# Keys and queries of the first image copied from SBUF, and the residuals of the second layer loaded inside the block and summed in place

## The chip, the core and the metric

The kernel runs on one core of a Trainium2 chip. The metric is the device time of one execution in microseconds (us); less is better. The core has TensorE (PE, matrix products, with its weight loads shown apart as PEld), VectorE (DVE), ScalarE (ACT), GpSimd (POOL) and SyncE (SP). They run side by side, each through its own list of instructions in order, and wait for one another through semaphores. Transfers are issued from SP's and POOL's lists here, and a few from ACT's at the very start.

## What is computed

Two attention layers, one after the other, over 4 images of 64 x 64 positions (4096 tokens) with 256 channels, in float32. Cut to what matters:

```python
def layer0(x):                       # x: (4, 4096, 256)
    q, k, v = x @ Wq + bq, x @ Wk + bk, x @ Wv + bv      # widths 32, 32, 256
    attn = softmax(einsum('bnd,bmd->bnm', q, k), axis=-1)
    return gamma * einsum('bnm,bmc->bnc', attn, v) + x

def layer1(x):
    f, g, v = x @ Wf + bf, x @ Wg + bg, x @ Wh + bh      # widths 32, 32, 128
    beta = softmax(einsum('bqd,bkd->bqk', g, f), axis=-1)
    return x + (einsum('bqk,bkd->bqd', beta, v) @ Wo + bo)
```

## The kernel before

`fast_path` does the work; `general_path` is a fallback behind a flag and does not run here.

**Projections.** A block is 512 tokens, 8 per image. `project_units(b, l, j)` gives a list of small functions for block j of image b in layer l: transpose the tokens, project q and k (`qk_unit`, tile psqk), project v (`v_unit`, tile psv). To keep precision with the faster number type, a value is split into a high and a low part. `qk_unit` leaves q and k of a block in one SBUF tile, `qk_parts`, of 128 rows: high q, high k, low q, low k, 32 rows each. The pool holds one such tile. Line 428 writes it to DRAM (`qk_dram`), from SP.

**Repeating rows.** The score matmul contracts over 128 rows, which are q and k repeated: q as high, high, low, low and k as high, low, high, low, so that one matmul sums all four products. `load_q` (lines 465 to 470) and `load_k` (lines 472 to 477) read these 32-row pieces from `qk_dram` with four transfers of 64 KB each, issued from POOL. A k tile is kept for each of the 8 blocks; there are two q tiles.

**Steps.** The main loop runs over `Step`s. In the first layer 256 queries stand against 512 keys in a step: 16 blocks of queries with 8 steps each. In the second layer 512 queries stand against 256 keys: 8 blocks with 16 steps. `scores()` computes the score tile st, of which there is one, on PE (line 502), and its exponentials on ACT: p (line 514), and in split steps also high (line 512) with a small factor. `cut_low` and `cut_both` compute low (line 519) and d (line 524) on DVE. In the first layer every step is split, in the second layer steps 2, 7 and 12. `products_first` and `products_second` multiply by v into the acc tiles (lines 533 and 554). In the second layer DVE also sums p (p_sum, line 700). In the program, step n does the scores of step n+2 ahead of its own products.

**The end of a block.** `end_first` gives the residual functions of the first layer: they write the new x to DRAM twice, as x1_dram for the next transposes and as x1_res with the output bias added. `end_second` (line 597) gives the output functions of the second layer for a block of 512 queries. Before: `begin` loads two pieces of the residual x1_res (128 tokens each, tile x_old, line 612) from SP, an empty function follows, and then four times `output(t)`: a matmul with Wo and one with ones (tile pso, lines 623 and 624), a reciprocal (line 626), y from pso and x_old (line 628), a transfer to the output (line 630), and the load of residual t+2. All of these tiles come from `small`, a ring of four buffers which x_res and x_new of the first layer share. The side tiles in PSUM (psqk, psv, pso) share two buffers.

**Pacing.** These functions form the list `units` and are spread over the steps of the next block: by step i of a second-layer block, ceil(len(units) * (i + 1) / 11) of them are done (line 704), in the first layer over 7 steps. In image b's second layer the projections of image b+1 are appended to the same list.

**The start.** The first `AHEAD` = 3 blocks of image 0 are projected ahead of the loop, with `load_k` after each and `load_q` after the first. The other five are projected within the first five steps (lines 689 to 720), `load_k` coming after the projection.

**The order of instructions.** The tile framework reorders what the program says: for each engine it makes a list of its own, from its picture of when tiles are ready. So an edit that makes a tile ready earlier, or shortens `units`, moves instructions of other engines too.

Of the kernel before, what the change touches and what calls it, by code (L numbers as in the profile page):

```python
# [50 lines left out]
F32R = mybir.dt.float32r  # L51
I32 = mybir.dt.int32
AF = mybir.ActivationFunctionType
ALU = mybir.AluOpType
AX = mybir.AxisListType

P = 128
QB = 512
QB0 = 256
NT = QB // P  # L60
# [3 lines left out]
AHEAD = 3  # L64
# [169 lines left out]
def fast_path(ctx: ExitStack, tc: tile.TileContext, x, w0, w1, wo, bo, gamma, out, off):  # L234

    nc = tc.nc
    B, N, C = x.shape
    NCC = C // P
    NB = N // QB
    D = w0[0].shape[1]  # L240
# [5 lines left out]
    NI = (N // (G[0] * P), N // (G[1] * P))  # L246
# [56 lines left out]
    inverse = const.tile([P, 2, B * N // P], F32, name="inverse")  # L303
# [39 lines left out]
    for j in range(NB):  # L343
        forms = {}
        for what, col in (("h", 1.0), ("l", 0.0), ("d", -EPS)):
            t = const.tile([P, NT, W], F32R, name=f"v0{what}_{j}")
# [19 lines left out]
    xT, x_parts, k_t, v_t = {}, {}, {}, {}  # L366
    qk_dram, x1_dram, x1_res = {}, {}, {}
    q_t = {}
# [36 lines left out]
    def project_units(b, l, j):  # L405
        key = (b, l, j)

        def qk_unit():
            ps = side_psum(f"psqk_{b}_{l}_{j}")
            for c in range(NCC):  # L410
                for n in range(2):
                    nc.tensor.matmul(  # L412
                        ps,
                        wqk[l][:, c, :],
                        x_parts[key][c][n],
                        start=(c == n == 0),
                        stop=(c == NCC - 1 and n == 1),
                    )
            whole = data.tile([2 * D, QB], F32, tag="qk", name=f"qk_{b}_{l}_{j}")
            parts = data.tile([P, QB], F32R, tag="qk_parts", name=f"qk_parts_{b}_{l}_{j}")  # L420
            top, bottom = slice(0, 2 * D), slice(2 * D, P)
            nc.scalar.copy(whole, ps[bottom, :])  # L422
            nc.vector.scalar_tensor_tensor(whole, ps[top, :], bqk[l], whole, ALU.add, ALU.add)  # L423
            nc.scalar.copy(parts[top, :], whole)
            nc.vector.tensor_sub(parts[bottom, :], whole, parts[top, :].bitcast(F32))

            qk_dram[key] = dram.tile([2, 2, D, QB], F32, name=f"qk_dram_{b}_{l}_{j}")
            nc.sync.dma_start(qk_dram[key].rearrange("h w d n -> (h w d) n"), parts.bitcast(F32))

        per = QB // CV[l]  # L430

        def v_unit(t0):
            def issue():
                ps = side_psum(f"psv_{b}_{l}_{j}_{t0}").rearrange("p (t c) -> p t c", c=CV[l])
                for t in range(per):
                    for c in range(NCC):
                        nc.tensor.matmul(  # L437
                            ps[:, t, :],
                            xT[key][:, c, (t0 + t) * P : (t0 + t + 1) * P],
                            wv[l][:, c, :],  # L440
                            start=(c == 0),
                            stop=(c == NCC - 1),
                        )
                tiles = slice(t0, t0 + per)
                seen = [seen_v[:, l, b * NB + j, n : n + 1] for n in range(2)]
                if l == 0:
                    split_values(ps, *(v0[j][what][:, tiles, :C] for what in ("h", "l", "d")), seen[t0 // per])
                    return
                for n in range(NT // G[1]):
                    i = j * NT // G[1] + n  # L450
                    v = ps[:, n * G[1] : (n + 1) * G[1], :]
                    if split[1][i]:
                        t = data.tile([P, 3, G[1], P], F32R, tag="v1_parts", bufs=sum(split[1]), name=f"v_{b}_{i}")
                        v_t[b, i] = {what: t[:, m] for m, what in enumerate(("h", "l", "d"))}
                        split_values(v, *v_t[b, i].values(), seen[n])
                    else:
                        v_t[b, i] = data.tile([P, G[1], P], F32, tag="v1", bufs=V1, name=f"v_{b}_{i}")
                        nc.scalar.copy(v_t[b, i], v)
                        nc.scalar.activation(v, v, AF.Abs, accum_out=seen[n])

            return issue

        return [transpose_unit(b, l, j), qk_unit] + [v_unit(t0) for t0 in range(0, NT, per)]

    def load_q(b, l, j):

        q_t[b, l, j] = data.tile([P, QB], F32R, tag="q", bufs=2, name=f"q_{b}_{l}_{j}")
        for n in range(4):
            src = qk_dram[b, l, j][n // 2, 0].bitcast(F32R)
            nc.gpsimd.dma_start(q_t[b, l, j][n * D : (n + 1) * D, :], src)  # L470

    def load_k(b, l, j):

        k_t[b, l, j] = data.tile([P, QB], F32R, tag="k", bufs=NB, name=f"k_{b}_{l}_{j}")
        for n in range(4):
            src = qk_dram[b, l, j][n % 2, 1].bitcast(F32R)
            nc.gpsimd.dma_start(k_t[b, l, j][n * D : (n + 1) * D, :], src)  # L477

    def nothing():
        pass  # L480
# [1 line left out]
    def small(name):  # L482
        return work.tile([P, C], F32, tag="small", bufs=4, name=name)
# [79 lines left out]
    def end_first(b, j, acc):  # L563
# [30 lines left out]

        return [residual(0), residual(1)]

    def end_second(b, j, acc, p_sum):
        key = f"{b}_{j}"
        o = []
        for h in range(QB // QB0):  # L600
            part = slice(h * QB0, (h + 1) * QB0)
            o.append(work.tile([P, W], F32, tag="o", name=f"o_{key}_{h}"))
            nc.scalar.activation(o[h][:, :QB0], acc[0][:, part], AF.Copy, scale=1.0 + EPS)
            nc.vector.tensor_add(o[h][:, :QB0], o[h][:, :QB0], acc[1][:, part])
        sums = work.tile([P, QB], F32, tag="sums", bufs=1, name=f"sums_{key}")
        nc.vector.tensor_add(sums, p_sum[:, :QB], p_sum[:, QB:])
        x_old = {}

        def load(t):
            if t < NT:  # L610
                x_old[t] = small(f"x1_old_{key}_{t}")
                nc.sync.dma_start(x_old[t], x1_res[b, j][t * P : (t + 1) * P, :])

        def begin():
            load(0)
            load(1)

        def output(t):
            def issue():
                tok = slice(t * P, (t + 1) * P)  # L620
                ps = side_psum(f"pso_{key}_{t}")
                part = o[t // NS][:, t % NS * P : (t % NS + 1) * P]
                nc.tensor.matmul(ps[:, :C], part, wo_sb, start=True, stop=True)  # L623
                nc.tensor.matmul(ps[:, C : C + 1], sums[:, tok], ones[:, :1], start=True, stop=True)  # L624
                n = (b * N + j * QB) // P + t
                nc.vector.reciprocal(inverse[:, 1, n : n + 1], ps[:, C : C + 1])
                y = small(f"y_{key}_{t}")
                nc.vector.scalar_tensor_tensor(y, ps[:, :C], inverse[:, 1, n : n + 1], x_old[t], ALU.mult, ALU.add)  # L628
                row = j * QB + t * P
                nc.sync.dma_start(out[b, row : row + P, :], y)  # L630
                load(t + 2)

            return issue

        return [begin, nothing] + [output(t) for t in range(NT)]

    def run(units):
        for u in units:
            u()


    x_res = {}
    for j in range(AHEAD):
        run(project_units(0, 0, j))
        load_k(0, 0, j)
        if j == 0:
            load_q(0, 0, 0)

    steps = [Step(b, l, j, i) for b in range(B) for l in range(2) for j in range(NQ[l]) for i in range(NI[l])]
    steps[0].scores()  # L650
# [7 lines left out]
    for n, s in enumerate(steps):  # L658
        b, l, j = s.b, s.l, s.j
# [14 lines left out]
        if l == 0 and s.last:  # L674
            x_res[b, j] = []
            for t in range(NS):
                x_res[b, j].append(small(f"x_res_{b}_{j}_{t}"))
                row = (j * NS + t) * P
                nc.sync.dma_start(x_res[b, j][t], x[b, row : row + P, :])
                nc.gpsimd.tensor_add(x_res[b, j][t], x_res[b, j][t], bv)  # L680

        ahead = steps[n + 3] if n + 3 < len(steps) else None
        if ahead is not None and ahead.first:
# [5 lines left out]
        early = []  # L689
        if b == l == j == 0 and s.i + AHEAD < NB:  # L690
            early = project_units(0, 0, s.i + AHEAD)
# [17 lines left out]
        if l == 1:  # L709
            later.scores()  # L710
            run(todo)
            s.products_second(acc)
        else:
            for half, what in ((0, "h"), (0, "l"), (1, "h")) if s.last else ((0, "h"), (1, "h")):
                s.products_first(acc, half, what)
            for half in () if s.last else (0, 1):
                s.products_first(acc, half, "l")
            run(early[1:])
            if early:
                load_k(0, 0, s.i + AHEAD)  # L720
            later.scores()
            run(todo)
            for half, what in ((0, "d"), (1, "l"), (1, "d")) if s.last else ((0, "d"), (1, "d")):
                s.products_first(acc, half, what)
# [76 lines left out]
```

## Time and profile before

| | us |
|---|---|
| median of 3 runs | 3236.67 (3235.38 to 3236.88) |
| the profiled execution | 3232.45 |
| its span, from first to last instruction | 3230.6 |
| mean granted clock of PE | 0.997 of full |

Busy time of PE in the span is 3166.9 us. The costliest groups and some that matter here, one row each from the groups by line:

| line, engine, tile | number | mean ns |
|---|---|---|
| 514 ACT p | 1024 | 1020 |
| 512 ACT high | 608 | 1116 |
| 519 DVE low | 608 | 1329 |
| 524 DVE d | 608 | 1255 |
| 700 DVE p_sum | 480 | 1223 |
| 623 PE pso with Wo | 256 | 380 |
| 470 POOL issue of q | 256 | 503 |
| 477 POOL issue of k | 256 | 499 |

Transfers from issue to landing, median: x_old from x1_res 2.1 us (128 times, 128 KB), qk_dram from qk_parts 2.1 (64 times, 256 KB), k and q from qk_dram 2.1 each (256 times, 64 KB).

How to read it: a matmul's end is modelled and matmuls are pipelined, so a busy PE can hold short waits; the distance between starts in the timeline tells more. "Idle before" names the engine whose work ended a wait last. Starts are in us from the beginning of the span.

### The profile page before, as it was taken

The page shows a single profiled execution, that of the slowest core. Times are in us where ns is not written, and L with a number is a line of the kernel's source. Part 1 is how long each engine was busy: PE and PEld are TensorE (multiplying, and loading weights), DVE is VectorE, ACT ScalarE, POOL GpSimd, SP SyncE. Part 2 cuts the span into 40 slices and gives each one's busy share as a digit, 9 for nine tenths or more (in the row PEclk, how much of TensorE's full clock was granted, in tenths as well). Part 3 has the DMA queues.
Part 4 walks back from the last instruction along what each step waited for, and adds up shares of the span by engine and source line. Part 5 has one row for each costly group of instructions (what it writes and reads, how often), then busy time and mean ns, then how long its engine had stood idle before and what let it go on. Part 6 is the DMA issues. An engine that isn't in the chain of part 4 may idle for free. (4 is left out here: it accounts for less than half of the span.)

```text
span 3230.6 us, 51123 instructions
## 1 busy us (share of the span) xinstructions
PE 3166.9 (98%) x19460; PEld 2616.2 (81%) x19460; DVE 2686.0 (83%) x3181; ACT 1989.2 (62%) x2483; POOL 660.7 (20%) x784
## 2 busy tenths in 40 slices
PE   8999999999999999999999999999999999999998
PEld 6999997565699999656679999966668999995554
DVE  6788888888888888888888888878888888887776
ACT  6666666555566666565556666655555666665554
POOL 2222223000222222300022222310002222241000
PEclk9999999999999999999999999999999999999999
DMA  4112123222212112322121212222222211121111
GB/s 116 41 50 50 43 57 74 58 53 49 63 44 56 42 47 51 77 56 51 48 64 44 50 46 54 60 66 53 49 54 61 53 44 47 43 71 47 33 33 36
DMA packets 368652, 172.15 MB, mean 53 GB/s; under 512 B 257392, under 2 KB 343664, under 8 KB 368400
## 3 DMA queue, kind: packets, MB, share of 16 engines
q1 hardware_dynamic: 342528, 134.29, 16.0%
q0 software_dynamic: 24960, 34.18, 4.4%
q8 instruction: 157, 2.57, 0.3%
q14 instruction: 95, 0.78, 0.1%
q10 hardware_dynamic: 912, 0.33, 0.0%
HBM read 101.58 MB, written 67.11 MB: 52 GB/s over the span
## 5 line engine op out<-in xcount | busy, mean ns | idle before, releaser
L514 ACT ACTIVATE p<-st 128x1024 f32<-128x1024 f32 x1024 | 1044.5, 1020 | 386.3 <-PE st L502 380.1
L512 ACT ACTIVATE high<-st,down 128x1024 fp32r<-128x1024 f32 x608 | 678.7, 1116 | 691.4 <-PE st L502 571.0
L524 DVE SCALAR_TENSOR_TENSOR d<-low,high 128x1024 fp32r<-128x1024 f32 x608 | 762.9, 1255 | 208.7 <-PE acc L533 203.3
L519 DVE TENSOR_TENSOR low<-p,high 128x1024 fp32r<-128x1024 f32 x608 | 807.8, 1329 | 140.9 <-ACT p L514 140.9
L554 PE MATMUL acc<-p,v 128*128 128x512 f32 x1664 | 789.3, 597 | 0.0
L502 PE MATMUL st<-q,k 128*128 128x256 f32 (+1 forms) x3072 | 775.8, 361 | 11.7 <-ACT p L514 11.5
L700 DVE TENSOR_TENSOR p_sum<-p_sum,p 128x1024 f32<-128x1024 f32 x480 | 586.8, 1223 | 58.8 <-ACT p L514 50.8
L502 PEld LDWEIGHTS st<-q,k 128*128 128x128 f32 x3072 | 463.3, 189 | 208.4 <-ACT p L514 115.1
L533 PE MATMUL acc<-v0d,d 128*128 128x258 f32 x4096 | 592.3, 284 | 0.1
L533 PE MATMUL acc<-v0h,high 128*128 128x258 f32 x4096 | 588.6, 284 | 3.1 <-ACT high L512 3.0
L533 PE MATMUL acc<-v0l,low 128*128 128x258 f32 x4096 | 588.3, 283 | 2.3 <-DVE low L519 2.3
L533 PEld LDWEIGHTS acc<-v0h,high 128*128 128x128 f32 x4096 | 533.8, 190 | 5.3 <-ACT high L512 3.8
L533 PEld LDWEIGHTS acc<-v0d,d 128*128 128x128 f32 x4096 | 533.9, 190 | 4.8 <-DVE d L524 1.6
L533 PEld LDWEIGHTS acc<-v0l,low 128*128 128x128 f32 x4096 | 533.0, 190 | 3.9 <-DVE low L519 3.7
L554 PEld LDWEIGHTS acc<-p,v 128*128 128x128 f32 x1664 | 308.7, 190 | 226.0 <-issue 198.9
L590 POOL TENSOR_TENSOR x_res<-x,bo 128x256 f32<-128x256 f32 x128 | 215.2, 1681 | 858.6 <-DVE g L580 480.1
L470 POOL DMA_DIRECT2D q<-qk_dram x256 | 125.9, 503 | 1165.5 <-PE st L502 1145.1
L680 POOL TENSOR_TENSOR x_res<-x_res,bv 128x256 f32<-128x256 f32 x128 | 190.1, 1486 | 149.9 <-DMA x_res<-in_x 102.8
L437 PE MATMUL psv<-wv,xT 128*128 128x128 f32 (+1 forms) x1024 | 191.1, 330 | 7.5 <-DVE qk L423 6.7
L477 POOL DMA_DIRECT2D k<-qk_dram x256 | 125.1, 499 | 300.6 <-DMA qk_dram<-qk_parts 158.4
L437 PEld LDWEIGHTS psv<-wv,xT 128*128 128x128 f32 x1024 | 159.0, 192 | 29.6 <-DVE qk L423 9.3
L388 DVE TENSOR_TENSOR xl<-xT,xh 128x512 fp32r<-128x512 f32 x128 | 87.0, 683 | 4.0 <-ACT xh L387 3.7
(94 smaller groups left out, 1676.7 us busy)
## 6 DMA issues: line engine op xcount, KB each, us to landing
x_res<-in_x SPq DMA_DIRECT2D x128, 128.0 KB, 2.2
qk_dram<-qk_parts SPq DMA_DIRECT2D x64, 256.0 KB, 2.1
k<-qk_dram POOLq DMA_DIRECT2D x256, 64.0 KB, 2.1
q<-qk_dram POOLq DMA_DIRECT2D x256, 64.0 KB, 2.1
x_dram<-x SPq DMA_DIRECT2D x128, 128.0 KB, 1.7
x_res<-x_res SPq DMA_DIRECT2D x128, 128.0 KB, 1.7
squares<-x_dram SPq DMA_DIRECT2D x256, 64.0 KB, 2.3
x_old<-x_res SPq DMA_DIRECT2D x128, 128.0 KB, 2.1
```

Source lines behind the costliest of these rows:

```text
L437: nc.tensor.matmul(ps[:, t, :], xT[key][:, c, (t0 + t) * P : (t0 + t + 1) * P], wv[l][:, c, :], start=(c == 0), stop=(c == NCC - 1),)
L470: nc.gpsimd.dma_start(q_t[b, l, j][n * D : (n + 1) * D, :], src)
L502: nc.tensor.matmul(st[:, g, :], k_t[b, l, kt // NT][:, kt % NT * P : (kt % NT + 1) * P], q_t[b, l, j * n // QB][:, q0 : q0 + n], start=Tru ...
L512: nc.scalar.activation(self.high, s_flat, AF.Exp, bias=down)
L514: nc.scalar.activation(self.p, s_flat, AF.Exp)
L519: nc.vector.tensor_sub(self.low, self.p, self.high.bitcast(F32))
L524: nc.vector.scalar_tensor_tensor(self.d, self.low.bitcast(F32), -1.0 / EPS, self.high.bitcast(F32), ALU.mult, ALU.add)
L533: nc.tensor.matmul(acc[2 * s + which][:, :W], p[:, g * QB0 + s * P : g * QB0 + (s + 1) * P], v0[self.i][v][:, g, :], start=self.first and ...
L554: nc.tensor.matmul(acc[which], v[:, g, :], p[:, g * QB : (g + 1) * QB], start=first and g == 0, stop=last and g == G[1] - 1,)
L590: nc.gpsimd.tensor_add(x_old[s], x_new[s], bo_sb)
L680: nc.gpsimd.tensor_add(x_res[b, j][t], x_res[b, j][t], bv)
L700: nc.vector.tensor_add(p_sum, p_sum, s.p)
```

## The change

It has three parts.

1. For image 0 in the first layer, `qk_unit` itself calls `load_k` (and for block 0 `load_q`) right after the write to DRAM, with the tile `qk_parts` as the source in place of `qk_dram`. The write to DRAM stays; q tiles of later blocks are still read from it. The calls of `load_k` and `load_q` ahead of the loop and in it go. The two functions share a helper, `load_rows`.
2. In the second layer the four pieces of the residual are loaded by `load_old`, called at step 12 of 16 of the block that they belong to, in place of the loads at the end. `begin`, the empty function and the loads in `output` go, so that `end_second` gives four functions and not six.
3. y has no tile of its own: it is written over the residual, and goes out from there.

```diff
+            if b == l == 0:
+                near = parts.rearrange("(h w d) n -> h w d n", h=2, w=2)
+                load_k(b, l, j, near)
+                if j == 0:
+                    load_q(b, l, j, near)
...
-    def load_q(b, l, j):
-
+    def load_rows(dst, parts, which, halves):
+        for n, h in enumerate(halves):
+            nc.gpsimd.dma_start(dst[n * D : (n + 1) * D, :], parts[h, which])
+
+    def load_q(b, l, j, parts=None):
         q_t[b, l, j] = data.tile([P, QB], F32R, tag="q", bufs=2, name=f"q_{b}_{l}_{j}")
-        for n in range(4):
-            src = qk_dram[b, l, j][n // 2, 0].bitcast(F32R)
-            nc.gpsimd.dma_start(q_t[b, l, j][n * D : (n + 1) * D, :], src)
+        load_rows(q_t[b, l, j], qk_dram[b, l, j].bitcast(F32R) if parts is None else parts, 0, (0, 0, 1, 1))
...
+    def load_k(b, l, j, parts=None):
         k_t[b, l, j] = data.tile([P, QB], F32R, tag="k", bufs=NB, name=f"k_{b}_{l}_{j}")
...
+        load_rows(k_t[b, l, j], qk_dram[b, l, j].bitcast(F32R) if parts is None else parts, 1, (0, 1, 0, 1))
...
+    def load_old(b, j):
+
+        x_old[b, j] = []
+        for t in range(NT):
+            x_old[b, j].append(small(f"x1_old_{b}_{j}_{t}"))
+            nc.sync.dma_start(x_old[b, j][t], x1_res[b, j][t * P : (t + 1) * P, :])
...
-        x_old = {}
-
-        def load(t):
-            if t < NT:
-                x_old[t] = small(f"x1_old_{key}_{t}")
-                nc.sync.dma_start(x_old[t], x1_res[b, j][t * P : (t + 1) * P, :])
-
-        def begin():
-            load(0)
-            load(1)
+        y = x_old.pop((b, j))
...
-                y = small(f"y_{key}_{t}")
-                nc.vector.scalar_tensor_tensor(y, ps[:, :C], inverse[:, 1, n : n + 1], x_old[t], ALU.mult, ALU.add)
+                nc.vector.scalar_tensor_tensor(y[t], ps[:, :C], inverse[:, 1, n : n + 1], y[t], ALU.mult, ALU.add)
                 row = j * QB + t * P
-                nc.sync.dma_start(out[b, row : row + P, :], y)
-                load(t + 2)
+                nc.sync.dma_start(out[b, row : row + P, :], y[t])
...
-        return [begin, nothing] + [output(t) for t in range(NT)]
+        return [output(t) for t in range(NT)]
...
     for j in range(AHEAD):
         run(project_units(0, 0, j))
-        load_k(0, 0, j)
-        if j == 0:
-            load_q(0, 0, 0)
...
+        if l == 1 and s.i == NI[1] - 4:
+            load_old(b, j)
...
             run(early[1:])
-            if early:
-                load_k(0, 0, s.i + AHEAD)
             later.scores()
```

More of the change, by code (lines that the diff above doesn't have):

```diff
@@ L463, in project_units @@
         return [transpose_unit(b, l, j), qk_unit] + [v_unit(t0) for t0 in range(0, NT, per)]
-    def load_q(b, l, j):
+    def load_rows(dst, parts, which, halves):
+        for n, h in enumerate(halves):
+            nc.gpsimd.dma_start(dst[n * D : (n + 1) * D, :], parts[h, which])
+    def load_q(b, l, j, parts=None):
         q_t[b, l, j] = data.tile([P, QB], F32R, tag="q", bufs=2, name=f"q_{b}_{l}_{j}")
-        for n in range(4):
-            src = qk_dram[b, l, j][n // 2, 0].bitcast(F32R)
-            nc.gpsimd.dma_start(q_t[b, l, j][n * D : (n + 1) * D, :], src)
-    def load_k(b, l, j):
+        load_rows(q_t[b, l, j], qk_dram[b, l, j].bitcast(F32R) if parts is None else parts, 0, (0, 0, 1, 1))
+    def load_k(b, l, j, parts=None):
         k_t[b, l, j] = data.tile([P, QB], F32R, tag="k", bufs=NB, name=f"k_{b}_{l}_{j}")
-        for n in range(4):
-            src = qk_dram[b, l, j][n % 2, 1].bitcast(F32R)
-            nc.gpsimd.dma_start(k_t[b, l, j][n * D : (n + 1) * D, :], src)
+        load_rows(k_t[b, l, j], qk_dram[b, l, j].bitcast(F32R) if parts is None else parts, 1, (0, 1, 0, 1))
     def nothing():
@@ L639, in run @@
             u()
-    x_res = {}
+    x_res, x_old = {}, {}
     for j in range(AHEAD):
         run(project_units(0, 0, j))
-        load_k(0, 0, j)
-        if j == 0:
-            load_q(0, 0, 0)
     steps = [Step(b, l, j, i) for b in range(B) for l in range(2) for j in range(NQ[l]) for i in range(NI[l])]
```

## The prediction

> **What bounds the kernel now.** I read the page's busy shares first, then the waits of PE, then busy time by 20 us stretches, then the timeline where stretches have holes.
>
> ```profile
> PE 3166.9 (98%) x19460; PEld 2616.2 (81%) x19460; DVE 2686.0 (83%) x3181; ACT 1989.2 (62%) x2483; POOL 660.7 (20%) x784
> ```
>
> TensorE is the bound: 63.7 us of the span are without a matmul. Which stretches hold them:
>
> ```profile
> 0.00:20.00 20.00, 11.91 (x41) 7.75 (x42) 10.34 (x68) 9.82 (x19) 9.51 (x20) 1.00 0.72 205
> 20.00:40.00 20.00, 17.05 (x83) 13.21 (x82) 12.77 (x19) 14.42 (x27) 8.81 (x19) 0.91 0.51 143
> 60.00:80.00 20.00, 17.75 (x108) 15.43 (x107) 13.97 (x18) 13.48 (x26) 2.86 (x6) 1.00 0.17 50
> 80.00:100.00 20.00, 15.49 (x88) 13.55 (x87) 11.54 (x16) 10.33 (x17) 3.87 (x8) 0.91 0.15 43
> ```
>
> The second figure is PE's busy time. The first 100 us lack 17.8 us in all; the start of each image's second layer lacks about 6 us, the end 13; the rest lacks under 0.3 per stretch. So a gain can come from the start, from the end, or from block edges of the second layer.
>
> ```profile
> PE acc L554 <- DVE d L524: 13.9, 33, 1.5
> PE st L502 <- ACT p L514: 11.5, 14, 1.7
> PE psv L437 <- DVE qk L423: 6.7, 5, 1.8
> ```
>
> No wait of PE names a DMA of q, k or x_old. The score tile st has one buffer, so scores of step n+1 wait for p of step n. That is the chain that appears here.
>
> The way of the first image's keys, block 0 and then block 7 (timeline):
>
> ```profile
> 16.49 0.33 SPq L428 DMA_DIRECT2D qk_dram<-qk_parts  x1
> ...
> 21.03 1.95 POOL L470 DMA_DIRECT2D q<-qk_dram  x4
> ...
> 31.47 0.82 PE L502 MATMUL st<-q,k 128*128 128x256 f32 x4
> ...
> 87.77 0.32 SPq L428 DMA_DIRECT2D qk_dram<-qk_parts  x1
> ...
> 90.25 1.93 POOL L477 DMA_DIRECT2D k<-qk_dram  x4 [6.87 <-DMA qk_dram<-qk_parts]
> ...
> 95.45 0.92 PE L502 MATMUL st<-q,k 128*128 128x256 f32 x4
> ```
>
> Block 7's parts are written at 87.77, read at 90.25 to 92.18, land 2.1 later (page, part 6) near 94.3, and the last scores of the row start at 95.45. ACT idles 5.52 us before their exponential. A block edge, second layer, image 0, blocks 0 to 1:
>
> ```profile
> 581.29 0.71 PE L502 MATMUL st<-q,k 128*128 128x512 f32 x2
> 581.84 0.40 PE L554 MATMUL acc<-low,v 128*128 128x512 f32 x1
> 582.08 0.28 PE L624 MATMUL pso<-ones,sums 128*128 128x1 f32 x2
> 583.17 0.73 PE L502 MATMUL st<-q,k 128*128 128x512 f32 x2 [0.82 <-ACT p L514]
> ```
>
> Between two scores there is too little other matmul work, and PE waits 0.82. The end:
>
> ```profile
> 3217.11 0.42 SPq L612 DMA_DIRECT2D x_old<-x_res  x1
> ...
> 3217.85 0.48 DVE L628 SCALAR_TENSOR_TENSOR y<-pso,inverse,x_old 128x256 f32<-128x256 f32 x1
> ...
> 3219.36 0.48 DVE L628 SCALAR_TENSOR_TENSOR y<-pso,inverse,x_old 128x256 f32<-128x256 f32 x1 [1.02 <-DMA x_old<-x_res]
> ```
>
> [...] 2.1 us to landing for the 256 KB write and for the 64 KB reads alike. [...] in a block of the second layer PE shows 98 to 99% busy, and adding up its work leaves about 1 us of 41.6 idle. [...] in the last stretch shown (clock 0.91): eight acc matmuls from 93.73 take 1.72 us, against 0.97 from 106.10. [...]
>
> **The change part by part.** The scheduler's order in the built program of the changed kernel differs in three places; it is the same, row for row, in the rest of the first layer and in the tail on PE and ACT.
>
> *Start.* q and k of image 0 are copied from qk_parts, not from DRAM. The DRAM write stays (later q tiles read it). Same number of DMAs. For block 0 POOL is free of its two x_res additions at 17.05 (15.18 plus 1.87), so eight issues at 0.5 end at 21.0 and land at 23.1, against 22.98 plus 2.1, or 25.1. The order uses this: the first scores now stand right after the transposes that end at 24.86, before the projection of block 2; no wait, 1.7 us in hand. Laying the durations of these rows along the new order, PE has by 37.8 done the same transposes and in addition 23 acc matmuls at 0.12: a lead of 2.8 us, from work that fills the holes of 1.3 (before 26.17) and others. It varies between 2.2 and 3.6 over the next blocks. For block 7, psqk ends 3.6 earlier, but the exponentials of step 6 (2.0) now stand ahead of the cast of qk_parts on ACT, so the parts are ready about 2.0 earlier; without the write the reads begin 90.25 - 87.77 = 2.5 earlier still. k lands 4.5 earlier, and the last scores, which followed it by 1.2 on the throttled clock, come 4.5 to 5.5 earlier. After that both orders are equal. I take 5.0. New waits: the next block's qk_parts (one buffer) must now wait for the reads. Block 1's cast ran at 22.94; the reads land at 23.1. ACT is held 0.2, and behind it stands v0h, which waited for PE until 24.46 anyway. Later blocks have about 10 us. That a DMA out of 32 SBUF rows costs the same as out of DRAM is not in the trace; bounds are 1 us less [...] and 1.5 more, and 1.5 is covered for block 0 but not for block 7. So 2.5 to 7.5.
>
> *Block edges.* Dropping the two empty units, and having residuals loaded, moves each output two steps forward: pso of output 0 stands behind the second scores of a block, not the fourth. Total work is equal; what counts is the sum over steps of the larger of PE's work and the loop from scores to scores. Prices from start distances in the timeline: scores 0.46, a full p step 1.72, high, low and d 0.47 each, pso 0.43 plus 0.14, psqk 0.235, psv 0.43. The loop is 0.46, 0.2 to ACT's start, 1.02 for p and 0.06: 1.74; with high ahead of it 2.75. For the block after block 0 the old order puts 2.19, 2.62, 1.74, 0.84 behind scores 1 to 4, the 0.84 being the hole above; the new one 1.76, 2.90, 1.76, 1.97. The sums over the 16 steps are 40.37 and 39.43: 0.94 less; in the last image 35.99 and 34.97, 1.02 less. Following actual starts instead (the old ones from scores 2 at 576.24 to scores 11 at 600.06 take 23.8, for 22.2 of work) gives up to 1.6. I take 1.3, four times: 5.2. For blocks 2 to 7 the sums are 41.06 and 41.15, since step 7 falls to 2.66 against its loop of 2.75: 0.09 more, 18 times: 1.6 lost. In the last image 36.68 both ways. Bounds for this pair: 2 to 6 gained, and 4 lost to 2 gained.
>
> *Residuals.* The same 128 loads and additions, in place, no instruction more. On SP each load of the next block waits for the output of the same buffer to land (2.1), and the next output stands behind it. These are 2 us or more apart on DVE anyway. Behind them stand four loads of squares, which go out at 677.93 in block 3 now; the last y ends at 673.87, so its output lands and the load behind it is out before 677. Cost nothing; the transpose that needs them starts at 686.6, and beyond that cover the excess is paid once per block. At the second layer's start two more loads (0.4 each) precede squares, whose own wait ended at 544.06, with SP free from 538.9. Nothing.
>
> *End.* The last residual is there, so the last y follows the one before it: 3217.85 plus 0.4 instead of 3219.36. 1.1 saved; the final checks, in a chain behind it, move along.
>
> Sum: -5.0 - 5.2 + 1.6 - 1.1 = -9.7. The profiled execution took 3232.45 (span 3230.6), so 3222.7; it was 4.2 below the median of 3236.67, which becomes 3227.0.
>
> **Rivals.** *Given back.* If the scores put early only displace projections, and the last k of the row turns out no nearer to its scores, the start gives nothing: -4.7, 3232.0. For it: from 40 to 60 us PE is 100% busy. Against: the 2.5 us at block 7 are on the chain, with ACT idle 5.5.
>
> *Slower.* DVE takes its queue in order, and the new order puts the reciprocal and y of outputs 0 and 1 ahead of low and d of step 2, each bound to a pso matmul. If one arrives late, low and d come late and PE waits at acc. By my sum d of step 2 ends 4.16 after the scores of step 3 and PE asks for it at 4.71: 0.55 in hand. If pso comes late and each of the 24 blocks from the third on loses 0.8 (the size of the wait shown at 583.17), that is +19.2, net +9.5, 3246.2. It cancels the gain from 0.40 a block, and makes the kernel slower than can be told from 0.68. For it: 33 waits of PE for d already. Against: DVE is 83% busy, idle 1.30 before low at 662.08, and y fits there.
>
> *Not as said.* That k and q are wrong or the loads stay where they were is excluded by the order on POOL and SP.
>
> **How the numbers follow.** Forecast 0.60, given back 0.18, slower 0.22. 0.2% is 6.5 us, about what a measurement can tell from no change. Within the forecast (own range 3220 to 3233) three quarters or more lie beyond 6.5: 0.48, and 0.12 within. Given back: 0.04 faster, 0.14 same. Slower: 0.02 same, 0.20 slower. Together 0.52, 0.28, 0.20. The range 3218 to 3243 leaves out about half of the slower case and a little at the bottom.
>
> **What would show it.** Start right: first scores near 25, k of block 7 issued near 86, its scores near 90, PE's busy time from 80 to 100 up by 3 us or more. Edges right: distance from the sums of block 0 to those of block 1 down from 40.99 by over 1; blocks 2 to 7 within 0.2 of 41.62. End right: no wait of y for x_old. It is wrong if scores wait for q or k, or if PE's waits for d grow beyond 13.9 us.

## The result and the profile after

The changed kernel takes 3223.07 us in the median of 6 runs (3222.18 to 3224.22), the kernel before 3236.03 (6 runs, 3232.84 to 3238.66). The medians differ by 13.0 us; the ratio is 0.9961, 95% interval 0.9948 to 0.9974: 8 to 17 us less, against 9.7 forecast. Beside the experiments below, the kernel before has medians of 3233.24 to 3233.90, and the change, timed again there, 3224.12, which is 9.1 less than the 3233.24 beside it. The two profiled executions stand 10.2 us apart in their spans (3230.6 and 3220.4). All sums by place below are of these two, so that they can be compared with the steps of the prediction.

The page's line of busy shares, after:

```profile
PE 3166.5 (98%) x19460; PEld 2613.0 (81%) x19460; DVE 2691.5 (84%) x3181; ACT 1988.8 (62%) x2483; POOL 661.3 (21%) x784
```

PE does the same 19460 matmuls in the same busy time. Everything that was won is time without a matmul, 53.9 us instead of 63.7. Where it was won, by stretches (length, busy time of PE, PEld, DVE, ACT and POOL with instruction counts, PE's granted clock, DMA share, GB/s):

```profile
0.00:20.00 20.00, 13.88 (x44) 9.12 (x44) 10.40 (x68) 9.79 (x19) 11.98 (x26) 1.00 0.72 212
20.00:40.00 20.00, 18.00 (x105) 15.28 (x104) 15.34 (x20) 15.37 (x29) 5.83 (x12) 1.00 0.48 136
60.00:80.00 20.00, 19.84 (x120) 17.30 (x119) 15.56 (x21) 15.87 (x30) 3.92 (x8) 1.00 0.20 53
80.00:100.00 20.00, 16.97 (x124) 15.69 (x124) 14.50 (x21) 13.28 (x20) 2.56 (x5) 1.00 0.11 27
```

Two things changed. PE is busier (most of all from 60 to 80 us, 19.84 against 17.75), and its clock is 1.00 in the two stretches that had 0.91. A stretch at a lower granted clock is called a dip from here on; the second of the two changes will turn out to be partly chance. The way of the keys, block 0 and then block 7 (timeline: start, duration, engine, line, tiles, and in brackets the wait before it):

```profile
15.84 2.00 POOL L472 DMA_DIRECT2D k<-qk_parts  x4
17.82 1.94 POOL L472 DMA_DIRECT2D q<-qk_parts  x4
...
24.18 0.72 PE L505 MATMUL st<-q,k 128*128 128x256 f32 x4
...
84.04 0.98 POOL L472 DMA_DIRECT2D k<-qk_parts  x2 [6.83 <-ACT qk_parts L424]
85.52 0.98 POOL L472 DMA_DIRECT2D k<-qk_parts  x2 [0.50 <-DVE qk_parts L425]
...
87.14 1.22 PE L536 MATMUL acc<-v0d,d 128*128 128x258 f32 x8 [1.24 <-DVE d L527]
88.38 0.71 PE L505 MATMUL st<-q,k 128*128 128x256 f32 x4
```

The first scores start at 24.18 (before 31.47), block 7's keys leave at 84.04 and 85.52 (90.25), the last scores of the row start at 88.38 (95.45). The copies now wait for the two engines that fill qk_parts, each for its half, and for no transfer.

As a clock for comparing starts I use one instruction, called M here: the exponential p of the first step of the second block of queries. In the timeline of ACT, after:

```profile
93.10 1.02 ACT L517 ACTIVATE p<-st 128x1024 f32<-128x1024 f32 x1
```

Before:

```profile
100.38 1.02 ACT L514 ACTIVATE p<-st 128x1024 f32<-128x1024 f32 x1
```

A block edge of the second layer shows in the starts of sums, which DVE computes once per block. Blocks 0 and 1 of image 0, before and then after:

```profile
573.84 0.68 DVE L606 TENSOR_TENSOR sums<-p_sum 128x512 f32<-128x512 f32 x1
614.83 0.69 DVE L606 TENSOR_TENSOR sums<-p_sum 128x512 f32<-128x512 f32 x1
...
566.08 0.69 DVE L616 TENSOR_TENSOR sums<-p_sum 128x512 f32<-128x512 f32 x1
606.27 0.69 DVE L616 TENSOR_TENSOR sums<-p_sum 128x512 f32<-128x512 f32 x1
```

The distance was 40.99 and is 40.19. The order of PE at such an edge and the end, after:

```profile
572.97 0.59 PE L624 MATMUL pso<-wo,o 128*128 128x256 f32 x2
573.45 0.73 PE L505 MATMUL st<-q,k 128*128 128x512 f32 x2
574.02 0.28 PE L625 MATMUL pso<-ones,sums 128*128 128x1 f32 x2
...
3209.32 0.48 DVE L628 SCALAR_TENSOR_TENSOR x_old<-pso,inverse,x_old 128x256 f32<-128x256 f32 x1
```

The pso matmuls stand two steps earlier, and the last sum no longer waits for its residual. From the last sums to the last y it was 7.94 us (3211.42 to 3219.36) and is 6.39 (3202.93 to 3209.32).

The waits of PE (us in total, times, longest):

```profile
PE acc L557 <- DVE d L527: 13.7, 32, 1.5
PE st L505 <- ACT p L517: 8.3, 10, 1.7
PE psv L442 <- DVE qk L423: 6.1, 4, 1.8
```

Hardly anything moved at d, 3.2 us went from the waits for p. No wait of PE for q, k or x_old appeared.

By place, from marks that both timelines have (M, the starts of sums, the last y), in us; negative is time won:

| place | forecast | profiled pair |
|---|---|---|
| start, up to M | -5.0 | -7.28 |
| rest of the first layer, image 0 | 0 | -0.48 |
| first edge of the second layer (sums of block 0 to sums of block 1), four images | -5.2 | -0.80 -0.83 -0.84 -0.94 = -3.41 |
| the six later distances, images 0 to 2 | +1.6 | +0.74 +0.77 +0.82 = +2.33 |
| the six later distances, image 3 | 0 | -1.20 |
| from an image's last sums to the next one's first | 0 | +0.22 +1.32 +0.02 = +1.56 |
| end | -1.1 | -1.55, and -0.13 behind the last y |
| sum | -9.7 | -10.2 |

The sum agrees, the terms do not. The experiments ask which of them are the change's.

### The profile page after: what moved, and what is told of

Its sections match the earlier page's. It is cut to its first block, busy times and chain, and to the rows that moved or that the text cites. A ratio compares the mean times of both kernels' runs of the same rounds, so it can differ in the third digit from the quotient of the medians.

```text
span 3220.4 us, 51144 instructions
## 1 busy us (share of the span) xinstructions
PE 3166.5 (98%) x19460; PEld 2613.0 (81%) x19460; DVE 2691.5 (84%) x3181; ACT 1988.8 (62%) x2483; POOL 661.3 (21%) x784
## 5 line engine op out<-in xcount | busy, mean ns | idle before, releaser
L472 POOL DMA_DIRECT2D k<-qk_dram x224 | 109.6, 500 | 245.2 <-PE st L505 140.3
```

The costliest lines, as they stand in the source:

```text
L472: nc.gpsimd.dma_start(dst[n * D : (n + 1) * D, :], parts[h, which])
```

## The experiments

All times are compared with the kernel before, run beside them. "Distance" is from one block's sums to the next one's in the second layer; the kernel before has 40.99, then 41.59 to 41.65 with 41.2 at the last, and 36.94, then 37.37 in the last image.

**1. The first part alone** (start_only): the near copies as in the change; outputs, empty units and residuals as before.

```diff
         y = x_old.pop((b, j))
-        return [output(t) for t in range(NT)]
+        return [begin, nothing] + [output(t) for t in range(NT)]
...
-        if l == 1 and s.i == NI[1] - 4:
-            load_old(b, j)
```

> Only the first part: q and k of the first image copied from SBUF; residuals, two empty units and outputs as before. In the profile of the full change the start is 7.3 us ahead at the first exponential of the second block (93.10 against 100.38). Theory 'three separate places': the same here, 93.1 give or take 0.4, block distances of the second layer back at 40.99 and 41.62, the last y again waiting for x_old; span near 3223, ratio near 0.9977. Rival 'given back': the lead at the start needs the other parts or is eaten later; then the lead shrinks before the last score and the ratio is 0.999 or more.

Ratio 0.9979 (0.9972 to 0.9987), median 3226.78. M at 93.43, first distance 41.00 to 41.01, 41.59 to 41.65 after it, last y 1.05 us late for x_old. As the first theory has it: the lead at the start is kept to the end, and it needs nothing of the other parts. The rival "given back" falls.

**2. The other parts alone** (ends_only): keys through DRAM, called where they were.

```diff
-            if b == l == 0:
-                near = parts.rearrange("(h w d) n -> h w d n", h=2, w=2)
-                load_k(b, l, j, near)
-                if j == 0:
-                    load_q(b, l, j, near)
...
             run(early[1:])
+            if early:
+                load_k(0, 0, s.i + AHEAD)
```

> Only the other parts: residuals loaded within the block, summed in place, no empty units; keys through DRAM as before. Theory 'three separate places': start as before (100.4), distance of the sums 40.19 for blocks 0 to 1, 41.75 after that, 37.17 in the last image, last y without a wait; -3.4 for the four first edges, +2.3 for 18 later ones, -1.2 for the last image, -1.5 at the end: 3.8 us less, ratio near 0.9988. Rival 'the edges only look better because the kernel entered them earlier': distances stay at 40.99 and 41.62.

Ratio 0.9986 (0.9980 to 0.9993). The distances are those of the change: 40.17 to 40.18 for the first, 41.73 to 41.77 after it (41.3 at the last), 37.15 to 37.18 in the last image, and no wait at the end. They don't depend on how the kernel entered them. But M was a surprise: 97.15, not 100.4, though nothing at the start differs from the kernel before: up to M the traces show the same instructions in the same order on every engine. Its stretches:

```profile
20.00:40.00 20.00, 17.03 (x91) 13.35 (x90) 14.29 (x19) 15.10 (x28) 8.35 (x18) 1.00 0.55 151
80.00:100.00 20.00, 15.37 (x98) 13.29 (x98) 12.33 (x16) 11.40 (x18) 3.32 (x7) 1.00 0.16 41
```

The clock is 1.00 in both. In the profile of the kernel before it was 0.91 in both, and its exponentials fall behind just there: 2.0 us by the first (0.44 of it from the first blocks' arrival), 1.2 more between steps 6 and 7. So 3.2 of the 7.28 us at the start may not be the change's.

**3. Is that chance?** (before_again): the kernel before, unchanged.

> The kernel before once more, unchanged, for a second profile. Theory 'two clock dips at the start of the first profile were chance': ends_only has the same order at the start and no dip, and comes at 97.15; so here the first exponential of the second block falls at 97 (no dip), near 98.5 (one) or 100.4 (two), with PE's order the same, while the block distances stay within 0.05 of 40.99, 41.62 and 37.37. Rival 'the start of the kernel before differs in its order': 100.4 again, within 0.3.

M at 99.07, between the two, with one of the two dips:

```profile
20.00:40.00 20.00, 17.04 (x83) 13.10 (x82) 13.05 (x19) 14.47 (x28) 8.72 (x19) 0.91 0.55 151
80.00:100.00 20.00, 15.38 (x95) 13.08 (x94) 12.47 (x16) 11.55 (x19) 3.89 (x8) 1.00 0.17 42
```

With one and the same order of instructions the start ends at 97.15, 99.07 or 100.38, in profiles with no dip, one and two up to there. The distances repeat to 0.05 us.

**4. The early call without the short way** (early_dram).

```diff
-                load_k(b, l, j, near)
+                load_k(b, l, j)
                 if j == 0:
-                    load_q(b, l, j, near)
+                    load_q(b, l, j)
```

> The full change, but the early calls for q and k read the DRAM copy again: same place in the program, one more DMA in each block's chain. Theory 'round trip': [...] k of block 7 is issued near 87 instead of 84.0, and the first exponential of the second block comes at 95.8 to 96.2. Rival 'order': what counts is that scores were put ahead of projections; then it stays within 0.5 of 93.1, and the first scores wait about 1 us for q. Rival 'nothing but the trip': it returns to 100.4.

M at 96.81, the clock at 1.00: 0.3 from ends_only, where the calls stand late. Up to M the order of instructions is the same in both traces, so the call's place in the program gives nothing; ratio 0.9990 (0.9983 to 0.9997), like ends_only. I had expected 95.8 to 96.2, from the dipped 100.38. The way of block 7's keys:

```profile
87.89 1.94 POOL L471 DMA_DIRECT2D k<-qk_dram  x4 [6.88 <-DMA qk_dram<-qk_parts]
92.17 0.63 PE L504 MATMUL st<-q,k 128*128 128x256 f32 x4
```

**5. Only block 7 from SBUF** (near_last), **6. only block 0** (near_first), **7. all but block 0** (near_not_first). The edit in each is the condition:

```diff
-                load_k(b, l, j, near)
+                load_k(b, l, j, near if j == NB - 1 else None)    # 5
+                load_k(b, l, j, near if j == 0 else None)         # 6
+                load_k(b, l, j, near if j else None)              # 7
...
-                    load_q(b, l, j, near)
+                    load_q(b, l, j)                               # 5 and 7
```

> The mirror image: q and k of blocks 0 to 6 through DRAM, k of block 7 alone copied from SBUF. Theory 'block 7 carries it': first exponential of the second block at 93 to 94.2, ratio to the kernel before near that of the full change, 0.9961 to 0.997. Rival 'block 0 carries it': 96 to 97.2 and a ratio near 0.998 to 0.999.

> The full change, but only block 0's q and k are copied from SBUF; k of blocks 1 to 7 is read from the DRAM copy, from the early place. The four profiles so far put the first exponential of the second block at 93.10, 93.43 and 93.88 with copies from SBUF for all blocks, and at 96.81 and 97.15 with all of them through DRAM (100.38 in the profile of the kernel before). Theory 'block 7 carries it': only the last block's keys are on the chain, so this one loses the gain and comes at 95.8 to 97.2. Rival 'block 0 carries it': the early scores fill PE's holes, and it comes at 93 to 94. If both carry it, near 95.

> The full change with block 0's q and k through DRAM and k of blocks 1 to 7 copied from SBUF. With block 7 alone from SBUF the first exponential of the second block came at 94.92, with all from SBUF at 92.34 to 94.28 (five profiles), with none at 96.81 and 97.15. Theory 'the early scores of block 0 only pay where the later blocks keep up': the middle blocks don't bind, so this one is like block 7 alone, 94.5 to 95.3. Rival 'the middle blocks carry what is left': 93 to 94.

| k from SBUF for blocks | M | clock 20:40, 80:100 | PE busy 60:80 | ratio |
|---|---|---|---|---|
| none (early_dram) | 96.81 | 1.00, 1.00 | 17.74 | 0.9990 (0.9983 to 0.9997) |
| 7 | 94.92 | 1.00, 1.00 | 17.74 | 0.9981 (0.9973 to 0.9990) |
| 1 to 7 | 92.83 | 0.94, 1.00 | 19.80 | 0.9968 (0.9956 to 0.9980) |
| 0 to 7 (the change) | 93.10 | 1.00, 1.00 | 19.84 | 0.9961 (0.9948 to 0.9974) |
| 0 | 101.21 | 1.00, 0.85 | 18.58 | 0.9993 (0.9986 to 1.0000) |

Block 7 alone brings 1.9 us, blocks 1 to 6 another 2.1, block 0 nothing, though its copies put the first exponential p of the kernel 6 us earlier (27.54 against 33.93 in near_not_first). Each M here is of one profile, and the four profiles with all copies and no dip up to M, equal in order, spread from 92.34 to 93.43; so 1.9 and 2.1 are rough, and near_not_first has a dip besides. The times give the same order. Those of near_not_first and of the change, taken side by side, are equal: 3224.11 and 3224.12 (6 runs each; the latter is after_again, below), so block 0 is worth nothing there too. My expectation for near_not_first was wrong: the middle blocks carry as much as the last. Block 7 alone:

```profile
84.97 0.49 POOL L472 DMA_DIRECT2D k<-qk_parts  x1 [3.92 <-ACT qk_parts L424]
85.69 1.45 POOL L472 DMA_DIRECT2D k<-qk_parts  x3 [0.23 <-DVE qk_parts L425]
89.86 0.63 PE L536 MATMUL acc<-v0l,low 128*128 128x258 f32 x3 [0.96 <-DVE low L522]
90.32 0.64 PE L505 MATMUL st<-q,k 128*128 128x256 f32 x4
```

Against early_dram the last copy is issued 2.7 us earlier (87.14 against 89.83, starts plus durations) and the scores come 1.85 earlier. They don't wait for the copy, which has landed at 88.70: they stand in PE's list behind three products with low, and these wait for DVE. The middle blocks act in PE's holes, in the row from 60 to 80, near_last and then near_not_first:

```profile
60.00:80.00 20.00, 17.74 (x111) 15.40 (x110) 14.06 (x18) 15.18 (x28) 2.84 (x6) 1.00 0.13 41
```

```profile
60.00:80.00 20.00, 19.80 (x121) 17.28 (x120) 15.37 (x21) 16.20 (x30) 3.91 (x8) 1.00 0.21 54
```

With the middle keys at hand, PE has matmuls for 2.06 us of holes in that stretch, and the projection of block 7 is done 2.3 us sooner. Block 0 alone is a trap, near_first:

```profile
90.82 1.94 POOL L472 DMA_DIRECT2D k<-qk_dram  x4 [9.23 <-DMA qk_dram<-qk_parts]
94.77 1.20 PE L505 MATMUL st<-q,k 128*128 128x256 f32 x4 [2.00 <-DMA k<-qk_dram]
```

Its first p comes at 26.97, 6 us ahead of early_dram, but by step 6 both stand at 87.5: the early scores displaced projections. Block 7's keys then leave 2.9 us later than in early_dram, the scores wait 2.00 for them, and the clock dips (0.85). This is "given back", in the only variant where it happens; how much of M's 101.21 is the dip was not separated, and the time of this variant can't be told from early_dram's (0.9993 and 0.9990, intervals overlap).

**8. The empty units put back** (empties_back), residuals still early.

```diff
-        return [output(t) for t in range(NT)]
+        return [nothing, nothing] + [output(t) for t in range(NT)]
```

> The full change with the two empty units put back ahead of the outputs; residuals still loaded early. Theory 'the place of the outputs sets the distances': they return to 40.99, 41.62 and 37.37, the end keeps its gain, because the residuals are there: total 1 to 2.5 us behind the full change's -10.2, so -8 to -9. Rival 'the loads and buffers set them': distances stay at 40.19, 41.75 and 37.17.

Distances 41.01 to 41.02, 41.62 to 41.65, 36.94 and 37.33 to 37.36 again; from the last sums to the last y still 6.39. Ratio 0.9975 (0.9965 to 0.9985). So the place of the outputs alone sets the distances, and the early loads, with the sum in place, which was not tried apart, give the end.

**9. Residuals called in the last step** (late_old).

```diff
-        if l == 1 and s.i == NI[1] - 4:
+        if l == 1 and s.last:
```

> The full change with the four residual loads issued in a block's last step instead of four steps from its end. Theory 'the loads have cover, it is the place of the outputs that counts': the last y still has its residual or waits under 0.5 us, distances stay at 40.18, 41.75 and 37.17, time within 1 us of the full change. Rival 'what stands behind a late y on DVE decides' (the slower case of the forecast): the first y of a block waits for its residual, low and d behind it come late, and the distances grow by 0.5 to 1 us in each of 32 blocks, 15 to 30 us in all.

Distances 40.18, 41.75 to 41.77 and mostly 37.20, ratio 0.9966 (0.9952 to 0.9980), as the first theory has it; but it is no test of a late residual. SP's own list, late_old:

```profile
3180.10 0.32 SPq L605 DMA_DIRECT2D x_old<-x_res  x1
3184.21 0.34 SPq L630 DMA_DIRECT2D out<-x_old  x1
3185.93 0.32 SPq L605 DMA_DIRECT2D x_old<-x_res  x1
```

The last four loads leave 29 to 10 us ahead of the last sums (3204.25), the one at 3180.10 for instance 24.1 ahead, as its counterpart in the change (3178.81 and 3202.93). Each follows the output that used its buffer, 1.7 us later in the lines above. In both programs a load goes out when the ring has a buffer for it, and moving the call by three steps changed nothing. What a residual that comes late would cost wasn't tried.

**10. A mixture** (spare_some): empty units where the table by place shows a loss.

```diff
+        spare = [nothing, nothing] if 0 < j < NB - 1 and b + 1 < B else []
-        return [output(t) for t in range(NT)]
+        return spare + [output(t) for t in range(NT)]
```

> The full change with the two empty units put back only where they were better: for the outputs that run in blocks 2 to 7 of images 0 to 2. Theory 'the place of the outputs sets the distances': 40.18 for the first edge, 41.62 after it, 37.17 in the last image, so 18 times 0.13, or 2.3 us, less than the full change. Rival 'the distances depend on the block before': blocks 2 to 7 stay at 41.75 and nothing is won.

Distances as expected: 40.15 to 40.18, then 41.58 to 41.65, 37.17. Ratio 0.9957 (0.9943 to 0.9971), median 3220.93. Once more, beside the change itself on one chip:

> The full change once more, timed beside the next run. Theory 'near copies shorten the start by about 4 us and keep PE's clock up there': first exponential of the second block at 92.3 to 94.3, clock 1.00 from 80 to 100 us; median 3222 to 3224. Rival 'chance': a profile with a dip there, beyond 95.

> The version with empty units for blocks 2 to 7 of images 0 to 2 once more, beside the full change on the same chip: theory says 2.3 us less than the full change, 3220 to 3222 in the median; rival 'no difference that can be told': within 1 us of it.

The change: 3224.12 (6 runs, 3222.70 to 3224.73), ratio 0.9969 (0.9957 to 0.9981), M at 93.60. The mixture: 3222.38 (5 runs, 3219.41 to 3225.85), 0.9964 (0.9950 to 0.9977). The medians differ by 1.7, which is the expected direction, but the ranges overlap: the 2.3 us are shown by the distances and not by the times. It is faster than the kernel before, and the best version here if there is a best one.

## Why the prediction was right, and where it was not

The time fell on the forecast's side by about the forecast's amount, and in part by luck. Without dips the terms add up to -7.8: -4.0 at M (below), -3.41, +2.33, -1.20 and -1.55. The edges were forecast 1.8 too high, the last image's gain was not foreseen, and dips of the clock, which differ from one execution to the next (two and one of them up to M in the two profiles of the kernel before), can make up the rest; that they do is not shown term by term. Of the prediction's own signs two were not met. PE's busy time from 80 to 100 us rose by 1.5 (15.49 to 16.97), not by 3 or more; from 60 to 80 us, where no sign was set, it rose by 2.1. And the first edge fell by 0.80 to 0.94, not by over 1. Its four steps, in its own order:

*Start, forecast -5.0.* The direction and the order of size are right, the division is wrong, in three terms. First, "a lead of 2.8 us" from block 0's early scores: near_not_first shows that they are worth nothing at M. Second, block 7's keys: "k lands 4.5 earlier" and all of it counted at the scores; alone they bring 1.9. The last scores did not follow the landing of k. The prediction adds the 2.1 to the end of the last issue (94.3), but the trace counts from its start, so k had landed at 93.73. The scores at 95.45 stood in PE's list behind these products, in the kernel before:

```profile
92.20 1.73 PE L533 MATMUL acc<-v0l,low 128*128 128x258 f32 x8 [0.95 <-DVE low L519]
93.73 1.92 PE L533 MATMUL acc<-v0d,d 128*128 128x258 f32 x8
```

Third, the middle blocks, which I didn't price at all ("Later blocks have about 10 us" was only about the buffer of qk_parts): they bring 2.1. That a copy out of 32 SBUF rows takes 1 us less to 1.5 more than a read from DRAM was my guess, from no trace; the copies of k landed after 2.1 in the median, as the reads do. In the profiles with the clock at 1.00 throughout the first 100 us, M falls at 92.34, 93.10, 93.18 and 93.43 with all copies from SBUF and at 96.81 and 97.15 with none, means 93.01 and 96.98: the change is worth 4.0 there. The profiled pair shows 7.28 because the profile of the kernel before had two dips. I took its lower clock (0.91 from 80 to 100 us), "1.2 on the throttled clock", for a property of the program; it was one of this execution (1.00 in before_again). As a mean it wasn't far off: over all profiles M stands at 93.40 with all copies (seven) and 98.35 without (four), 4.95 apart. At the very start the clock dips with and without the copies (three of seven profiles with all copies, at 18 to 19 us; two of four without, at 28). From 80 to 100 us it is 1.00 in all seven, and 0.91 in one of the four without. That dips are rarer there with the copies would fit the larger gain in the times (start_only 6.7 us in the median against 4.0) and the narrower spread (3222.18 to 3224.73 over 12 runs of the change, 3231.39 to 3238.66 over the runs of the kernel before beside them). It isn't proved by them.

*Block edges, first one, forecast -5.2.* The mechanism is right (empties_back). The size isn't: 0.80 to 0.94 for each edge, where the sum over steps said 0.94 and 1.02 and I raised it to 1.3 after "following actual starts". The sum of work was the better guide. The busy time agrees with it: between the sums of blocks 0 and 1 of image 0 PE was busy for 39.92 of 40.99 us in the kernel before and for 39.95 of 40.19 after, so 1.07 us were idle and 0.24 are.

*Blocks 2 to 7, forecast +1.6.* Right in sign: 0.13 for each, not 0.09, so 2.3. In the last image "36.68 both ways" failed: each distance falls by 0.20. In its block 4, three steps that took 2.51, 2.18 and 3.85 between exponentials (steps 9 to 11) take 1.86, 2.84 and 3.19, 0.65 less, while the steps up to there lose 0.44. My step model moved work between steps but did not see that the long step before the split one shrinks when its pso has gone.

*Residuals, forecast nothing.* Right. The loads wait 1.7 us for the output of the same buffer to land, and one y alone waits for one, 0.3 us.

*End, forecast -1.1:* 1.55, as the fourth residual no longer follows the second output.

*What wasn't in the sum.* +1.56 us between images. It is a dip of the clock in block 0 of the second layer, the same hole in image 0 and in image 2 of the changed kernel:

```profile
551.10 0.73 PE L557 MATMUL acc<-d,v 128*128 128x512 f32 x2 [1.54 <-DVE d L527]
551.67 1.02 PE L557 MATMUL acc<-p,v 128*128 128x512 f32 x2
...
2140.25 1.18 PE L557 MATMUL acc<-d,v 128*128 128x512 f32 x2 [1.54 <-DVE d L527]
2141.23 1.91 PE L557 MATMUL acc<-p,v 128*128 128x512 f32 x2
```

The wait in brackets is equal; after it the two rows of image 2 take 1.6 and 1.9 times as long as those of image 0. The clock is 0.50 from 2140.32 to 2143.73 us, and 1.00 from 551.17 to 554.58. From the exponential p of the first step of block 0 to that of block 1 it is 51.4 us in image 0 where no dip falls and 52.9 to 53.1 where one does, so about 1.6 us by chance. The profile of ends_only has such a dip in images 0 to 2, that of the kernel before in image 1 alone (0.50 from 1352.19 us on). The 0.48 us in the first layer of image 0 are no dip: start_only has them too, gained at the starts of block 3 and block 7, so they belong to the near copies; how they come about stays unexplained.

*Rivals.* "Given back" is excluded for the change by start_only, which keeps its lead (ratio 0.9979). "Slower" is excluded by the profile: d's waits are 13.7 us in 32 places, not more, though blocks 2 to 7 do lose a little to their new order. "Not as said" is excluded by the timelines.

## What to carry to other kernels

An earlier first result isn't a shorter start: follow it to the point where both orders are equal again, since the early scores of near_first were given back in full by step 6. Shortening a chain for all its links was worth about twice what it was for the last link, because the earlier links fill the holes ahead of it. And before a difference of a few us is put down to an edit, compare the granted clock in the same stretches, and take a second profile of the unchanged kernel.

## What the runs showed of the hardware

A copy of 64 KB from 32 rows of SBUF to 32 others lands 2.1 us after its issue in the median of the 32 copies of k, as the read of the same rows from DRAM does (2.1). Not all do: the four copies of q, issued from 17.82 us on, took 3.5 to 3.8, while the DMA share from 18 to 20 us was 0.95. What the near copies of k save is the wait for the write to DRAM, which itself lands after 2.1.

High, low and d are the values in the faster number type. In the timeline of the kernel before their products in a step take PE 0.46 to 0.47 us each (starts 595.16, 595.63, 596.09 and 596.55 us), those of p in float32 1.73 for the same 256 keys and 512 queries (602.65 to 604.84, less 0.46 for the scores in between).

Of two equal holes of PE, one is followed by 3.41 us at half the clock and the other isn't. In the changed kernel PE was idle for 1.83 us both from 547.76 to 551.17 (image 0) and from 2136.91 to 2140.32 (image 2); in the 3.41 us behind them the clock was 1.00 and 0.50. The same place can differ between two executions: from 80 to 100 us the kernel before had 0.91 in one profile and 1.00 in the other. In the first of these two, the dips ahead of the end are these (the figure ahead of the DMA share is the clock):

```profile
27.82:31.23 3.41, 3.41 (x10) 2.67 (x9) 0.70 (x2) 0.86 (x2) 3.08 (x7) 0.50 0.93 251
92.67:96.08 3.41, 3.41 (x18) 3.41 (x17) 0.74 (x1) 0.00 (x0) 0.00 (x0) 0.50 0.08 22
1352.19:1355.60 3.41, 2.88 (x5) 1.65 (x6) 3.41 (x5) 0.62 (x1) 0.63 (x2) 0.50 0.26 66
```

These three and the two of the changed kernel (from 1345.02 and 2140.32 us on) last 3.41 us each, at a clock of 0.50. In the 3.41 us ahead of them PE was idle for 1.48, 1.72, 1.48, 1.84 and 1.83 us; but the 1.83 us in image 0 of the changed kernel passed without a dip, so what makes one begin isn't shown. Each dip costs 1.2 to 1.6 us in the places measured above, and at most 1.7 by an estimate: half of 3.41 us, as the clock was 0.50. The two profiles of the kernel before differ by over 0.5 us in such places only (M, and block 0 of the second layer in image 0).
